# Layer 1 of a two-layer image kernel: four columns per transfer, even and odd columns apart in memory

## The chip, the cores and the metric

The kernel runs on one core of one Trainium2 chip. The metric is device time in microseconds (us). Before the change three runs took 5861.34, 5883.06 and 5891.94 us; their median, 5883.06 us, is the time before.

## What is computed

The input `x` has the shape (4, 64, 256, 256): batch, channels, height, width. Two layers follow each other, both with a residual:

```python
x = x + _L0_conv_ref(_gn(x), ...)   # layer 0
x = x + _L1_conv_ref(_gn(x), ...)   # layer 1
```

`_gn` is a group norm with 32 groups of two channels, over a whole image. Layer 0 is a pointwise convolution to 384 channels, a 3x3 convolution per channel, a product of q and k in the frequency domain of 8x8 patches, a layer norm over channels, a product with v, and a projection back to 64 channels. Layer 1 is a recurrence over the 256 columns of the image:

```python
def step(prev_col, cur_col):
    nb = jnp.concatenate([pad, prev_col, pad], axis=1)
    x = jnp.concatenate([nb[:, :-2], nb[:, 1:-1], nb[:, 2:]], axis=-1)
    new = _gru_cell(x.reshape(B * H, 3 * Cf), cur_col.reshape(B * H, Cf), w_ih, w_hh, b_ih, b_hh)
    return (new, new)
```

Each pixel's new state is that of a GRU cell. Its input is the states of three neighbouring pixels in the column before; its old state is the normalized pixel itself. Column 0 is passed on as it is. Column w needs column w-1, so the columns can only be worked off in order.

## The kernel before

All arithmetic is in float32. The width is the outer pixel dimension in memory, so that a column of 256 pixels of one channel is a run of 1 KB. Layer 0 writes its result to `x1`, a tensor in device memory of the shape [B, C, W, H] (line 185), and layer 1 reads it from there and writes `out` in the same layout.

*Order.* Nearly every instruction is recorded by the helper `InOrder` (line 145), which keeps each engine's instructions in program order. The profile therefore shows line 157 for almost everything, and groups are told apart by the names of their tiles. DMAs on the SP queue (`nc.sync.dma_start`) are issued in program order too: an instruction on SP that waits holds up all that come after it.

*Layer 0* (lines 271 to 694) runs over 32 blocks of the image. In each block, TensorE (PE) computes the hidden channels of the block (`pointwise`), applies matrices that are streamed in from `t_all` 24 times per block (`transform`, `values`; tile `t`, four buffers, SP queue), multiplies spectra on VectorE (tiles `pr`), and goes back (`inverse`). `finish` (line 608) gates and projects in four steps u: it loads the input again (tile `xr`, two transfers of 256 KB), adds the projection, takes statistics and stores the sum to `x1` by `store` (line 589), two transfers of 256 KB in runs of 512 B. The tiles `xr`, `pr`, `q`, `y` and `seen` share a pool of seven buffers (`wk`), so that a product may have to wait until a store of an `xr` has landed.

*Layer 1* (from line 717) holds columns in pieces of WB = 8. A column has 4 images x 64 channels; the 128 partitions hold two images at a time, and the second index (the slot) takes the other two. In even columns the slots hold images (0, 1) and (2, 3), in odd columns (0, 2) and (1, 3) (`SLOTS`, line 699). The pieces are

- `raw`: the columns as read, three buffers of 8 columns. `load_columns` (line 732) fetches two columns at a time, w and w+1: one transfer of 256 KB for the even column and two of 128 KB for the odd one, 16 columns ahead.
- `xn`: the columns normalized by ScalarE (ACT), `normalize` (line 748), one slot of one column in each half of a step, eight columns ahead. Before the loop it is done for nine columns.
- `xt`: the same with the halves of the partitions exchanged, made by two transfers of 128 KB each time two columns are normalized (the "turn").
- `st`: the states. `column` (line 801) computes a column in two parts along its height. The cut between the parts moves by one pixel per column, over 32 columns (`parts`, line 779), so that the first part of a column needs only the first part of the column before.

For each part, PE does the gates r, n and z (tiles `pshr`, `psni`, `pshz`, and `pshn` for both parts together) from `xn`, `xt` and the three shifted views of the previous `st`. `state` (line 838) then takes sigmoids and a tanh on ACT, and VectorE (DVE) combines them to the new state. GpSimd (POOL) adds the state to `raw` in place (`add`, line 767). After each odd column, `add` stores two columns to `out`: one transfer of 256 KB and two of 128 KB. The step then ends by loading two more columns. In SP's queue the order for each two columns is therefore: two turns, three stores, three loads.

Of the kernel before, what the change touches and what calls it, by code (L numbers as in the profile page):

```python
# [10 lines left out]
F32 = mybir.dt.float32  # L11
AF = mybir.ActivationFunctionType
ALU = mybir.AluOpType
# [3 lines left out]
B, C, W, H = 4, 64, 256, 256  # L17
HID = 6 * C
E = 2 * C
P = 128  # L20
NPAIR = B // 2
# [141 lines left out]
def tile_conv_then_gru(  # L163
# [17 lines left out]
    nc = InOrder(tc, tc.nc)  # L181

    const = ctx.enter_context(tc.tile_pool(name="const", bufs=1))
    dram = ctx.enter_context(tc.tile_pool(name="dram", bufs=1, space=DRAM))
    x1 = dram.tile([B, C, W, H], F32, tag="x1", name="x1")


    t_all = dram.tile([3, 8, HALO, 16 * NS], F32, tag="t_all", name="t_all")
# [28 lines left out]
    with tc.tile_pool(name="xa", bufs=3) as xa, tc.tile_pool(name="sta", bufs=1) as sta, tc.tile_pool(  # L217
        name="bps", bufs=1, space=PSUM
# [10 lines left out]
        for i in range(32):  # L229
            kind, s = i // 16, i % 16  # L230
            c0, num = 2 * P * kind, 2 * P - P * kind
            ps = banks[0:HALO, 4 * (i % 2) : 4 * (i % 2) + 4, 0:num]
            for k in range(4):
                at = slice(32 * k, 32 * k + 9)
# [25 lines left out]
    for a in range(2):  # L260
        at = slice(a * C, (a + 1) * C)
# [12 lines left out]
    with ExitStack() as s:  # L274
# [6 lines left out]
        place = [0]  # L281
# [307 lines left out]
        def store(n, u, xr):  # L589
            b, r0, c0 = n // 8, (n % 8) * 32 + (u // 2) * 8, (u % 2) * P  # L590
            for g in range(2):
                nc.sync.dma_start(
                    x1[b, :, r0 + 16 * g : r0 + 16 * g + 8, c0 : c0 + P],
                    xr[g * C : (g + 1) * C],
                )

        def look(n, k, t):

# [25 lines left out]
        for n in range(NBLK + 1):  # L624
# [13 lines left out]
            more = n // 8 + 1 < B  # L638
# [77 lines left out]

    WB = 8
    with ExitStack() as s:
        rawp = s.enter_context(tc.tile_pool(name="raw", bufs=3))
        colp = s.enter_context(tc.tile_pool(name="cols", bufs=2))  # L720
        gk = s.enter_context(tc.tile_pool(name="gk", bufs=2))
        ps_g = s.enter_context(tc.tile_pool(name="ps_g", bufs=1, space=PSUM))
        raws, xns, xts, stcols = {}, {}, {}, {}

        def columns(m, w):

            yield m[:, :, w, :].rearrange("(k a) c h -> (a c) k h", k=NPAIR), slice(0, P), 0
            for half in range(2):
                b0 = SLOTS[1][0][half]
                yield m[b0 : b0 + 2, :, w + 1, :].rearrange("b c h -> c b h"), slice(half * C, half * C + C), 1  # L730

        def load_columns(w):
            n, i = w // WB, w % WB
            if i == 0:
                raws[n] = rawp.tile([P, 2, WB, H], F32, tag="raw", name=f"raw_{n}")
            for of, at, j in columns(x1, w):
                nc.sync.dma_start(raws[n][at, :, i + j], of)

        def new_columns(n):
            xns[n] = colp.tile([P, 2, WB, H], F32, tag="xn", name=f"xn_{n}")  # L740
            xts[n] = colp.tile([P, WB, H], F32, tag="xt", name=f"xt_{n}")

        def empty_states(n):
            stcols[n] = st = colp.tile([P, 2, WB, H + 2], F32, tag="st", name=f"st_{n}")
            nc.gpsimd.memset(st[:, :, :, 0:1], 0.0)
            nc.gpsimd.memset(st[:, :, :, H + 1 : H + 2], 0.0)

        def normalize(w, slot):
            n, i = w // WB, w % WB
            if i == slot == 0:  # L750
                new_columns(n)
            nc.scalar.activation(
                xns[n][:, slot, i],
                raws[n][:, slot, i],
                AF.Identity,
                bias=sc1[:, w % 2, slot, 0:1],
                scale=sc1[:, w % 2, slot, 1:2],
            )
            if slot and i % 2:

                for half in range(2):
                    nc.sync.dma_start(
                        xts[n][half * C : (half + 1) * C, i - 1 : i + 1],
                        xns[n][(1 - half) * C : (2 - half) * C, half, i - 1 : i + 1],
                    )

        def add(w):
            n, i = w // WB, w % WB
            nc.gpsimd.tensor_tensor(
                raws[n][:, :, i], raws[n][:, :, i], stcols[n][:, :, i, 1 : H + 1], ALU.add  # L770
            )
            if i % 2:
                for of, at, j in columns(out, w - 1):
                    nc.sync.dma_start(of, raws[n][at, :, i - 1 + j])

        QUARTERS = ((0, 0), (0, 1), (1, 0), (1, 1))
        SKEW = 32

        def parts(w):


            at = H // 2 + SKEW // 2 - (w - 1) % SKEW
            return (0, at), (at, H)

        MAX = H // 2 + SKEW // 2

        def bank_pair(gate, w):
            return ps_g.tile([P, 2, 512], F32, tag=gate, name=f"ps{gate}_{w}")

        def quarters(ps, weights, rhs, start, stop):  # L790
            for r, c in QUARTERS:
                nc.tensor.matmul(
                    ps[c * C : (c + 1) * C, r],
                    lhsT=weights[r * C : (r + 1) * C],
                    rhs=rhs(r, c),
                    start=start,
                    stop=stop,
                    tile_position=(r * C, c * C),
                )

        def column(w):

            i, xn, xt, st = w % WB, xns[w // WB], xts[w // WB], stcols[(w - 1) // WB]

            def own(ps, gate, h0, h1, stop):

                quarters(
                    ps,
                    wh[:, gate, :],
                    lambda r, c: (xn[:, c] if r == c else xt)[r * C : (r + 1) * C, i, h0:h1],  # L810
                    True,
                    stop,
                )

            def taps(ps, gate, h0, h1, start):
                for t in range(3):
                    quarters(
                        ps,
                        wi[:, 3 * gate + t, :],
                        lambda r, c: st[r * C : (r + 1) * C, c, (w - 1) % WB, h0 + t : h1 + t],  # L820
                        start and t == 0,
                        t == 2,
                    )

            pn = bank_pair("hn", w)[:, :, 0:H]
            for part in range(2):
                h0, h1 = parts(w)[part]
                pr, pi, pz = (bank_pair(gate, f"{w}_{part}")[:, :, 0 : h1 - h0] for gate in ("hr", "ni", "hz"))
                own(pr, 0, h0, h1, False)
                taps(pr, 0, h0, h1, False)  # L830
                if part == 0:
                    own(pn, 2, 0, H, True)
                taps(pi, 2, h0, h1, True)
                own(pz, 1, h0, h1, False)
                taps(pz, 1, h0, h1, False)
                state(w, part, pn[:, :, h0:h1], pr, pi, pz)

        def state(w, part, pn, pr, pi, pz):
            h0, h1 = parts(w)[part]
            i, num = w % WB, h1 - h0  # L840
            xn, st = xns[w // WB], stcols[w // WB]
            g = gk.tile([P, 2, MAX], F32, tag=f"g{part}", name=f"g_{w}_{part}")[:, :, 0:num]
            n = gk.tile([P, 2, MAX], F32, tag=f"n{part}", name=f"n_{w}_{part}")[:, :, 0:num]
            z = gk.tile([P, 2, MAX], F32, tag=f"z{part}", name=f"z_{w}_{part}")[:, :, 0:num]
            nc.scalar.activation(g, pr, AF.Sigmoid, bias=b_rz[:, 0:1], scale=1.0)
            if w + WB < W:
                normalize(w + WB, part)
            nc.vector.scalar_tensor_tensor(n, pn, bias_sb[:, 5:6], g, ALU.add, ALU.mult)
            nc.vector.tensor_tensor(n, pi, n, ALU.add)

            nc.scalar.activation(z, pz, AF.Sigmoid, bias=b_rz[:, 1:2], scale=-1.0)
            nc.scalar.activation(n, n, AF.Tanh, bias=bias_sb[:, 2:3], scale=1.0)
            nc.vector.scalar_tensor_tensor(g, z, -1.0, xn[:, :, i, h0:h1], ALU.add, ALU.mult)
            nc.vector.tensor_tensor(n, n, z, ALU.mult)
            nc.vector.tensor_tensor(st[:, :, i, 1 + h0 : 1 + h1], n, g, ALU.subtract)

        for w in range(0, 2 * WB, 2):
            load_columns(w)
        for w in range(WB + 1):
            for slot in range(2):  # L860
                normalize(w, slot)
        empty_states(0)
        nc.vector.tensor_copy(stcols[0][:, :, 0, 1 : H + 1], xns[0][:, :, 0])
        for w in range(W):
            n, i = w // WB, w % WB
            if i == 0 and n + 1 < W // WB:
                empty_states(n + 1)
            if w:
                column(w)
            add(w)  # L870
            if i % 2 and w + 2 * WB < W:
                load_columns(w + 2 * WB - 1)


# [52 lines left out]
```

## Time and profile before

| | |
|---|---|
| median of three runs | 5883.06 us |
| profiled execution | 5869.95 us |
| its span, first to last instruction | 5868.2 us |
| granted TensorE clock, mean | 0.994 |
| end of layer 0's last projection on PE | about 4326 us |
| first load of `raw` issued | 4338.1 us |
| first matmuls of column 1 on turned columns | 4357.8 us |
| last add on POOL starts | 5858.9 us |

The profile lists, for each engine, its busy time and what ended its idle stretches. "Issue" stands for idle time in which an engine waited for nothing that the profile shows. PEld is PE's loading of weights, which lies beside the matmuls. A matmul in float32 appears as two records, so that the 92 matmuls of a column are 184 records. The granularity of the DMA lines is one packet; transfers on SP are `SPq`.

In layer 1, between 4400 and 5800 us, the DMA moved 160.97 MB in 151538 packets at a mean of 115 GB/s, 40.1% of the 16 engines' time on SP's queue and 1.7% on the instruction queue.

### The profile page before, as it was taken

Reading aid. Unit: us, or ns where it says so; the run is one execution under the profiler, and the core shown is the slowest. Engines: PE = TensorE matmul, PEld = TensorE weight load, DVE = VectorE, ACT = ScalarE, POOL = GpSimd, SP = SyncE. Lnnn points to the kernel's source line nnn. Section 1 sums busy time; section 2 is a strip of 40 time slices with the busy share of each in tenths; the row PEclk is TensorE's granted clock in tenths of the full one; section 3 lists DMA queues with packets and bytes.
Section 4 is the critical chain, followed back from the end, with each engine's and each line's share of the span. In section 5 each row is a group of like instructions: output and inputs, shape, how many; then the busy total and the mean of one; then the engine's idle time right before and its main releaser. Section 6 shows DMA issues by size and latency. Waiting matters only on the chain. (4 is left out here: it accounts for less than half of the span.)

```text
span 5868.2 us, 278629 instructions
## 1 busy us (share of the span) xinstructions
PE 5479.9 (93%) x127196; PEld 4762.6 (81%) x127196; DVE 4080.5 (70%) x9593; ACT 3475.4 (59%) x4604; POOL 500.8 (9%) x797
## 2 busy tenths in 40 slices
PE   2999999999999999999999999999979999999998
PEld 1878888888788878887888888878868888888888
DVE  2776777777767777777677767766667777776766
ACT  2556566665565656655655666556556666666655
POOL 0000000000000000000000000000002122222222
PEclk9999999999999999999999999999989999999999
DMA  8455555555555555555555454544444444444443
GB/s 225 135 156 147 151 151 155 154 142 152 157 147 154 150 151 159 141 150 159 150 152 150 140 143 126 142 139 125 137 114 116 116 116 117 115 117 113 116 114 81
DMA packets 561916, 818.04 MB, mean 139 GB/s; under 512 B 41353, under 2 KB 435373, under 8 KB 559677
## 3 DMA queue, kind: packets, MB, share of 16 engines
q1 hardware_dynamic: 520152, 633.59, 40.0%
q0 software_dynamic: 37776, 165.24, 9.5%
q8 instruction: 996, 16.32, 1.2%
q10 hardware_dynamic: 2808, 1.38, 0.1%
q14 instruction: 184, 1.50, 0.1%
HBM read 622.46 MB, written 144.05 MB: 131 GB/s over the span
## 5 line engine op out<-in xcount | busy, mean ns | idle before, releaser
L157 PEld LDWEIGHTS psring<-h,t 100*32 100x32 f32 x40960 | 1334.1, 115 | 294.0 <-issue 175.2
L157 PE MATMUL psring<-h,t 100*32 100x128 f32 x40960 | 1445.2, 274 | 105.9 <-issue 37.7
L157 PE MATMUL psring<-w_sb,xq 64*100 64x128 f32 x24576 | 1403.2, 271 | 55.7 <-POOL xq L157 40.2
L157 PEld LDWEIGHTS psring<-w_sb,xq 64*100 64x100 f32 x24576 | 1357.6, 164 | 117.0 <-issue 50.2
L157 ACT COPY h<-psring 100x1024 f32<-100x1024 f32 x1274 | 1205.5, 1027 | 161.4 <-PE psring L157 155.2
L157 DVE TENSOR_TENSOR pr<-psring,q 128x512 f32<-128x512 f32 (+1 forms) x576 | 463.3, 857 | 308.8 <-PE psring L157 234.8
L157 DVE BATCH_NORM_STATS2 lnst<-z 128x6 f32<-128x64 f32 x4096 | 545.4, 214 | 117.6 <-ACT z L157 117.6
L157 DVE TENSOR_TENSOR z<-z,lnm 128x1024 f32<-128x1024 f32 x512 | 612.7, 1218 | 8.8
L157 ACT COPY q<-psring 128x1024 f32<-128x1024 f32 x256 | 259.3, 1013 | 596.8 <-PE psring L157 358.9
L157 ACT ACTIVATE z<-pshz,b_rz 128x288 f32<-128x288 f32 (+7 forms) x510 | 242.6, 476 | 519.8 <-PE pshz L157 519.7
L157 PE MATMUL pshr<-st,wi 64*64 64x144 f32 (+7 forms) x12240 | 510.5, 270 | 34.9 <-issue 20.9
L157 PE MATMUL psni<-st,wi 64*64 64x144 f32 (+7 forms) x12240 | 510.4, 270 | 24.4 <-issue 22.4
L157 PE MATMUL pshz<-st,wi 64*64 64x144 f32 (+7 forms) x12240 | 510.8, 270 | 23.1 <-issue 21.9
L157 ACT COPY z<-psring 128x2048 f32<-128x2048 f32 x128 | 238.9, 1867 | 446.7 <-PE psring L157 441.7
L157 PE MATMUL psring<-pr,g_sb 32*64 32x512 f32 x8192 | 494.8, 594 | 5.7 <-issue 5.5
L157 ACT ACTIVATE y<-psring,ln_sb 128x512 f32<-128x512 f32 x512 | 372.5, 781 | 200.5 <-PE psring L157 197.0
L157 PEld LDWEIGHTS psni<-st,wi 64*64 64x64 f32 x12240 | 446.5, 133 | 45.5 <-issue 34.4
L157 PEld LDWEIGHTS pshr<-st,wi 64*64 64x64 f32 x12240 | 422.3, 133 | 52.3 <-issue 49.5
L157 DVE COPY h<-psring 100x1024 f32<-100x1024 f32 x262 | 320.3, 1223 | 198.7 <-PE psring L157 194.7
L157 PEld LDWEIGHTS pshz<-st,wi 64*64 64x64 f32 x12240 | 424.9, 133 | 37.3 <-issue 36.4
L157 DVE SCALAR_TENSOR_TENSOR g<-z,xn 128x288 f32<-128x288 f32 (+7 forms) x510 | 218.4, 428 | 311.9 <-ACT z L157 310.0
L157 POOL TENSOR_TENSOR raw<-raw,st 128x512 f32<-128x512 f32 x256 | 303.7, 1186 | 1146.0 <-ACT xn L157 548.1
(98 smaller groups left out, 7377.9 us busy)
## 6 DMA issues: line engine op xcount, KB each, us to landing
t<-t_all SPq DMA_DIRECT2D x768, 400.0 KB
xq<-in_xh POOLq DMA_DIRECT2D x128, 800.0 KB, 4.6
xr<-in_x SPq DMA_DIRECT2D x256, 256.0 KB
x<-xr SPq DMA_DIRECT2D x256, 256.0 KB
seen<-in_x POOLq DMA_DIRECT2D x192, 256.0 KB, 4.1
raw<-x SPq DMA_DIRECT2D x128, 256.0 KB
raw<-x SPq DMA_DIRECT2D x256, 128.0 KB
xt<-xn SPq DMA_DIRECT2D x256, 128.0 KB
```

Source lines behind the costliest of these rows:

```text
L157: return self.tc.keep_in_program_order(got(*args, **kwargs))
```

## The change

Layer 1 loads, stores and turns four columns at a time. `x1` and `out` get a leading index for even and odd columns, so that two even (or two odd) columns lie side by side, as a run of 2 KB per channel; the host puts `out` back in order. Layer 0's `store` writes even and odd columns with separate transfers, four of 128 KB in place of two of 256 KB. `raw` becomes seven buffers of four columns, in the order even, even, odd, odd (`place`), and `xn` and `xt` follow the same order. One load is 512 KB (two even columns) or 256 KB (two odd columns, half the images), and stores are alike; a turn is 256 KB. Loads and stores are written at one per kind and step, three steps of each four. Before the loop, four columns are normalized instead of nine, and the first five steps normalize two columns each.

```diff
-    x1 = dram.tile([B, C, W, H], F32, tag="x1", name="x1")
+    x1 = dram.tile([2, B, C, W // 2, H], F32, tag="x1", name="x1")
...
             for g in range(2):
-                nc.sync.dma_start(
-                    x1[b, :, r0 + 16 * g : r0 + 16 * g + 8, c0 : c0 + P],
-                    xr[g * C : (g + 1) * C],
-                )
+                at = r0 // 2 + 8 * g
+                for odd in range(2):
+                    nc.sync.dma_start(x1[odd, b, :, at : at + 4, c0 : c0 + P], xr[g * C : (g + 1) * C, odd::2])
...
-        rawp = s.enter_context(tc.tile_pool(name="raw", bufs=3))
+        rawp = s.enter_context(tc.tile_pool(name="raw", bufs=7))
...
+        def place(w):
+            return w % WB // 4 * 4 + w % 2 * 2 + w % 4 // 2
+
+        def columns(m, w, i):
             if i == 0:
+                of = m[0, :, :, w // 2 : w // 2 + 2, :]
+                return of.rearrange("(k a) c w h -> (a c) k (w h)", k=NPAIR), raws[w // 4][:, :, 0:2]
+            half = i - 1
+            b0 = SLOTS[1][0][half]
+            of = m[1, b0 : b0 + 2, :, w // 2 : w // 2 + 2, :]
+            return of.rearrange("b c w h -> c b (w h)"), raws[w // 4][half * C : half * C + C, :, 2:4]
+
+        def load_columns(w, i):
+            if i == 0:
+                raws[w // 4] = rawp.tile([P, 2, 4, H], F32, tag="raw", name=f"raw_{w // 4}")
+            of, to = columns(x1, w, i)
+            nc.sync.dma_start(to.rearrange("p k w h -> p k (w h)"), of)
+
+        def store_columns(w, i):
+            to, of = columns(out, w, i)
+            nc.sync.dma_start(to, of.rearrange("p k w h -> p k (w h)"))
...
-            if slot and i % 2:
+            if slot and i % 4 == 3:
...
                     nc.sync.dma_start(
-                        xts[n][half * C : (half + 1) * C, i - 1 : i + 1],
-                        xns[n][(1 - half) * C : (2 - half) * C, half, i - 1 : i + 1],
+                        xts[n][half * C : (half + 1) * C, i - 3 : i + 1],
+                        xns[n][(1 - half) * C : (2 - half) * C, half, i - 3 : i + 1],
                     )
...
         def add(w):
-            if i % 2:
-                for of, at, j in columns(out, w - 1):
-                    nc.sync.dma_start(of, raws[n][at, :, i - 1 + j])
+            raw = raws[w // 4][:, :, place(w) % 4]
+            nc.gpsimd.tensor_tensor(raw, raw, stcols[w // WB][:, :, w % WB, 1 : H + 1], ALU.add)
...
-            if w + WB < W:
-                normalize(w + WB, part)
+            for more in range(ahead(w - 1), ahead(w)):
+                normalize(more, part)
...
+        def ahead(w):
+            return min(2 * w + 4, w + WB + 1, W)
...
             add(w)
-            if i % 2 and w + 2 * WB < W:
-                load_columns(w + 2 * WB - 1)
+            if i >= 2:
+                store_columns(w - i, i - 2)
+            elif i == 0 and w:
+                store_columns(w - 4, 2)
+            if i < 3 and w - i + 2 * WB < W:
+                load_columns(w - i + 2 * WB, i)
+        store_columns(W - 4, 2)
```

In the last part of the diff, `i` is w modulo 4.

More of the change, by code (lines that the diff above doesn't have):

```diff
@@ L723, in tile_conv_then_gru @@
         raws, xns, xts, stcols = {}, {}, {}, {}
[L725 to L733, printed above, removed]
-            if i == 0:
-                raws[n] = rawp.tile([P, 2, WB, H], F32, tag="raw", name=f"raw_{n}")
-            for of, at, j in columns(x1, w):
-                nc.sync.dma_start(raws[n][at, :, i + j], of)
+        def place(w):
+            return w % WB // 4 * 4 + w % 2 * 2 + w % 4 // 2
+        def columns(m, w, i):
+            if i == 0:
+                of = m[0, :, :, w // 2 : w // 2 + 2, :]
[12 more added lines that the diff above has]
+            nc.sync.dma_start(to, of.rearrange("p k w h -> p k (w h)"))
         def new_columns(n):
@@ L752, in normalize @@
             nc.scalar.activation(
-                xns[n][:, slot, i],
-                raws[n][:, slot, i],
+                xns[n][:, slot, place(w)],
+                raws[w // 4][:, slot, place(w) % 4],
                 AF.Identity,
@@ L758, in normalize @@
             )
-            if slot and i % 2:
+            if slot and i % 4 == 3:
                 for half in range(2):
                     nc.sync.dma_start(
-                        xts[n][half * C : (half + 1) * C, i - 1 : i + 1],
-                        xns[n][(1 - half) * C : (2 - half) * C, half, i - 1 : i + 1],
+                        xts[n][half * C : (half + 1) * C, i - 3 : i + 1],
+                        xns[n][(1 - half) * C : (2 - half) * C, half, i - 3 : i + 1],
                     )
         def add(w):
[L768 to L771, printed above, removed]
-            if i % 2:
-                for of, at, j in columns(out, w - 1):
-                    nc.sync.dma_start(of, raws[n][at, :, i - 1 + j])
+            raw = raws[w // 4][:, :, place(w) % 4]
+            nc.gpsimd.tensor_tensor(raw, raw, stcols[w // WB][:, :, w % WB, 1 : H + 1], ALU.add)
         QUARTERS = ((0, 0), (0, 1), (1, 0), (1, 1))
@@ L801, in column @@
         def column(w):
-            i, xn, xt, st = w % WB, xns[w // WB], xts[w // WB], stcols[(w - 1) // WB]
+            xn, xt, st = xns[w // WB], xts[w // WB], stcols[(w - 1) // WB]
             def own(ps, gate, h0, h1, stop):
@@ L809, in own @@
                     wh[:, gate, :],
-                    lambda r, c: (xn[:, c] if r == c else xt)[r * C : (r + 1) * C, i, h0:h1],
+                    lambda r, c: (xn[:, c] if r == c else xt)[r * C : (r + 1) * C, place(w), h0:h1],
                     True,
@@ L852, in state @@
             nc.scalar.activation(n, n, AF.Tanh, bias=bias_sb[:, 2:3], scale=1.0)
-            nc.vector.scalar_tensor_tensor(g, z, -1.0, xn[:, :, i, h0:h1], ALU.add, ALU.mult)
+            nc.vector.scalar_tensor_tensor(g, z, -1.0, xn[:, :, place(w), h0:h1], ALU.add, ALU.mult)
             nc.vector.tensor_tensor(n, n, z, ALU.mult)
             nc.vector.tensor_tensor(st[:, :, i, 1 + h0 : 1 + h1], n, g, ALU.subtract)
-        for w in range(0, 2 * WB, 2):
-            load_columns(w)
-        for w in range(WB + 1):
+        def ahead(w):
+            return min(2 * w + 4, w + WB + 1, W)
+        for w in range(0, 2 * WB, 4):
+            for i in range(3):
+                load_columns(w, i)
+        for w in range(ahead(0)):
             for slot in range(2):
@@ L864, in tile_conv_then_gru @@
         for w in range(W):
-            n, i = w // WB, w % WB
-            if i == 0 and n + 1 < W // WB:
+            n, i = w // WB, w % 4
+            if w % WB == 0 and n + 1 < W // WB:
                 empty_states(n + 1)
@@ L921 @@
         args.append(nc.dram_tensor(f"in_{name}", v.shape, mybir.dt.from_np(v.dtype), kind="ExternalInput").ap())
-    args.append(nc.dram_tensor("out_0", (B, C, W, H), F32, kind="ExternalOutput").ap())
+    args.append(nc.dram_tensor("out_0", (2, B, C, W // 2, H), F32, kind="ExternalOutput").ap())
     with tile.TileContext(nc) as tc:
@@ L925 @@
     r = run_bass_kernel_spmd(nc, [feeds], core_ids=[0])
-    return np.ascontiguousarray(r.results[0]["out_0"].transpose(0, 1, 3, 2))
+    got = r.results[0]["out_0"].reshape(2, B, C, W // 2, H)
+    return np.ascontiguousarray(got.transpose(1, 2, 4, 3, 0).reshape(B, C, H, W))
```

## The prediction

> **What bounds the kernel now.** I read the page's busy shares and slices first, then what PE waits for in the stage that the change rewrites (layer 1, from 4358 us, where the first column starts, to the end), then the stretches around single waits, then SP's timeline. From the page:
>
> ```profile
> PE 5479.9 (93%) x127196; PEld 4762.6 (81%) x127196; DVE 4080.5 (70%) x9593; ACT 3475.4 (59%) x4604; POOL 500.8 (9%) x797
> DMA  8455555555555555555555454544444444444443
> q1 hardware_dynamic: 520152, 633.59, 40.0%
> q8 instruction: 996, 16.32, 1.2%
> ```
>
> PE is the bound in both layers. DMA is half busy on average, so its mean bandwidth binds nothing; only where transfers bunch can it matter. The waits of PE from 4358 us to the end (total us, times, longest):
>
> ```profile
> PE pshr L157 <- issue: 29.0, 60, 1.2
> PE pshz L157 <- issue: 28.7, 53, 1.2
> PE psni L157 <- issue: 22.4, 31, 1.7
> PE pshr L157 <- DMA xt<-xn: 14.1, 1, 14.1
> PE pshr L157 <- DVE st L157: 13.4, 7, 1.9
> ```
>
> PE hardly ever waits for data: 13.4 us at the seven turns of the skew, and once for the first turned columns. The largest item, 80 us in 144 waits, is "issue": nothing that the profile tracks was missing. Where they sit names them. From the middle of one such wait to the middle of the next, PE executes a multiple of 128 matmuls (columns: stretch, length, PE busy, matmuls, clock, DMA share, GB/s):
>
> ```profile
> 4894.57:4902.36 7.79, 7.60 (x256) 1.00 0.44 123
> 4902.36:4906.36 4.00, 3.79 (x128) 1.00 0.37 103
> 4906.36:4914.17 7.81, 7.62 (x256) 1.00 0.46 123
> 4914.17:4918.17 4.00, 3.82 (x128) 1.00 0.37 102
> ```
>
> 128 matmuls with their 128 weight loads are 256 instructions, and queue q8 moved 16.32 MB in 996 packets, 16.4 KB each: PE waits for its next block of instructions. Counting on in 128s gives 338 block ends between 4409 and 5800 us, 3.87 us of work apart; 140 of them have a wait. Whether one has it depends on the DMA share in the 4 us that end 1 us before it:
>
> ```profile
> 4880.80:4884.80 4.00, 3.59 (x130) 1.00 0.17 42
> 4884.57:4888.57 4.00, 4.00 (x151) 1.00 0.66 185
> 4901.25:4905.25 4.00, 3.82 (x136) 1.00 0.38 107
> 4978.78:4982.78 4.00, 4.00 (x145) 1.00 0.73 206
> ```
>
> The block end at 4885.80 has no wait, that at 4889.57 waits 1.08 us, at 4906.25 0.23 us, at 4983.78 1.18 us. Over all 338, with the share from half-microsecond stretches: share under 0.3, 66 ends, mean wait 0.01 us; 0.3 to 0.6, 197 ends, 0.15 us; over 0.6 (mean 0.68), 75 ends, 0.64 us. A busy DMA delays the block, and PE stands still. So what the change does to layer 1's time is what it does to the bunching of its transfers. SP's timeline (start, length, transfers):
>
> ```profile
> 4899.37 3.26 SPq L157 DMA_DIRECT2D xt<-xn  x2
> 4902.72 5.17 SPq L157 DMA_DIRECT2D out<-raw  x3
> 4907.95 2.25 SPq L157 DMA_DIRECT2D raw<-x  x3
> ```
>
> Each pair of columns brings eight transfers of 128 or 256 KB, held apart by waits: the two turns by ACT's two slots, the second and third store by POOL's add. No stretch of 4 us is fully busy.
>
> [...] loads of 1 KB packets filled the DMA at 257 GB/s (4340 to 4356 us), and 1 KB and 2 KB packets cost about 57 and 120 ns. Doubling the runs thus saves no DMA time.
>
> **The change part by part.** *Arithmetic of layer 1.* Same matmuls, VectorE operations and adds; nothing gained.
>
> *SP's issues.* Per four columns 16 become 8, at 0.52 to 0.64 us each. SP is not on the path, so nothing is gained directly.
>
> *Bunching.* Bytes are equal: 2560 KB (of 1024) per four columns, 10.2 us at 257 GB/s of a cycle of 4 x 5.88 = 23.5 us. But SP runs its queue in order and stops only where an instruction must wait. Loads wait for nothing recent (the pool now holds seven blocks, and the stores of a reused block lie eight columns back). So they don't stay in "their" step: SP's order is two turns, [add of column 3] odd store, odd store, even load, odd load, [add of column 2] even store, odd load, and again. After the add of column 3, 256+256+512+256 KB go out in four issues, some 2.5 us, for 5.1 us of DMA work. Three columns later, after the add of column 2, follow 512+256 KB and right behind them both turns of 256 KB, which were nearly ready: another 5.1 us. Taking the add to end 9.6 us after its column starts on PE, as for the column whose xt issues at 4899.37 and 4902.11 lie 2.45 and 5.2 us after its start, the second group starts about 5.8 us before the next first one. The two join to about 10.7 us of full DMA, then 12.8 us of quiet. There are 5.7 block ends per cycle after it is lengthened a little. An end has a share over 0.6 if its 4 us overlap the full stretch by 2.4 or more: 10.7 + 4 - 4.8 = 9.9 us of 23.5, or 2.4 ends; a share of 0.3 to 0.6 for 2.4 us, 0.6 ends. The wait at full share isn't shown. The lower bound is 0.64 us (share 0.68). The upper one continues the line from 0.15 (mean share 0.41) to 0.64 (0.68): 1.8 us per unit, 1.2 us at 1.0. I take 0.75, near the lower one, since a wait also lengthens the cycle and drains the queue. Then 2.4 x 0.75 + 0.6 x 0.15 = 1.89 us per cycle, and 64 cycles make 121 us for 80: **+41 us** (bounds +24 and +110).
>
> *Larger packets.* A block on an engine busy with 2 KB or 4 KB packets might wait longer. Against it: around the turns, 2 KB already, block ends wait no longer than around 1 KB loads. Priced at 0, inside the upper bound.
>
> *Start of layer 1.* PE idled 14.1 us for the first xt, behind 24 loads (15.05 us on SP). Twelve loads issue in 7 us, and ACT normalizes 4 columns first instead of 9 (8 x 0.59 us for 18). But the same 4 MB drain at 257 GB/s, and the first turn is 512 KB where the first pair was 256: 1 us more. Against slow issuing at the beginning this is -1 us (-4 to +1). ACT then does two columns a step for five steps: 0.59 us more between a part's two sigmoids; ACT idled 0.9 to 1.2 us there on PE. Hidden.
>
> *Tail.* One issue less after the last add: -0.6 us; 512 KB still go out.
>
> *Layer 0.* 256 stores of 256 KB become 512 of 128 KB: 0.6 us more SP per extra one, 4.8 us in a block of about 127 us. Behind them in SP's queue stand the next xr loads and four t fetches; PE waited only 15 us for t there. DMA is full in this stretch (216 to 276 GB/s from 1334 to 1340 us), so issuing later mostly doesn't land later. But VectorE's products already wait 68.4 us in 23 places for a store to land, and PE's inverse waits for them. I take 4 us (0, to 1 us in each of 31 blocks, 31).
>
> Sum: 41 - 1 - 1 + 4 = +43 us. On the profiled execution (5869.95 us, span 5868.2) that is 5913. That execution lies 13 us under the median of the runs; against the median, 5883 + 43 = **5926 us**.
>
> **The rivals.**
> 1. *Bunching costs* (the forecast): own range 5900 to 5990. Chance 0.50.
> 2. *Requests count, not bytes* (the other side, faster): if each transfer disturbs block fetches by its start, layer 1's waits go with its number, 1024 before, 512 after, and half of the 80 us goes: 5883 - 40 - 2 = 5841. It decides once the wait in full stretches stays under 0.4 us. For it: the quiet half of each cycle has no waits. Against: waits follow the share, which is bytes. 0.18.
> 3. *Neither*: the joined groups come apart, or the wait is capped, so that the sum stays near 80 us: 5883 - 2 + 4 = 5885. For it: POOL's add moves by a microsecond or two between columns. 0.20.
> 4. *The block waits for the whole queue*: it now reaches 2.6 us of work (1310 KB less 2.5 us of draining), on average some 1.3, before about 0.4. Then 0.9 us more in 2 ends a cycle, 115 us: 6040. Against: at 1337 us of layer 0 the queue was as deep and PE kept running. 0.12.
>
> **How the numbers follow.** About 0.5% (29 us) is what a measurement of this kernel can tell from no change; the three runs lie 0.5% apart. Slower by more: 0.38 of the first, all of the fourth, 0.05 of the third, 0.55. Faster: 0.14 of the second, 0.02 of the first, 0.16. The rest, 0.29, is within it. The range, 5845 to 5990, leaves out the fourth and the lower part of the second.
>
> **What would show it.** In layer 1, PE's "issue" waits near 120 us, in fewer places, longer ones above 1 us common; DMA slices unchanged in the mean, but stretches of 4 us at a share near 1.0 followed by some 12 us near 0; SP's transfers in two groups of four per four columns. Right at the start, the wait for xt stays within a few us of 14.1. In layer 0, the wait of pr for the stores of x grows by at most 30 us. The forecast is wrong if the issue waits fall below 80 us, or if PE waits for xt or raw in mid-layer.

## The result, and the profile after

The changed kernel took 5937.61 us (median of four runs, 5932.63 to 5953.08) beside 5879.14 us for the kernel before. The ratio is 1.0097, with a 95% interval from 1.0075 to 1.0118: slower by about 57 us.

The same lines of the page, changed kernel:

```profile
PE 5471.9 (92%) x127196; PEld 4774.2 (80%) x127196; DVE 4081.0 (69%) x9593; ACT 3472.0 (59%) x4604; POOL 499.3 (8%) x797
DMA  8455555555555555555555555545454433334442
q1 hardware_dynamic: 442328, 633.57, 39.8%
q8 instruction: 996, 16.32, 1.2%
```

PE does the same work in the same busy time, within 8 us. The DMA moves the same bytes in fewer packets, and its busy share has hardly moved. So neither work nor traffic was added; PE stands still longer. The waits of PE in layer 1, from 4381 us to the end (total us, times, longest):

```profile
PE pshr L157 <- issue: 45.0, 46, 2.1
PE psni L157 <- issue: 42.8, 35, 2.3
PE pshz L157 <- issue: 39.6, 42, 1.9
PE pshr L157 <- DVE st L157: 13.4, 7, 1.9
PE pshr L157 <- DMA xt<-xn: 11.6, 2, 11.2
PE pshn L157 <- issue: 2.0, 3, 0.8
```

The issue waits, at the ends of the instruction blocks, sum to 129 us in 126 places, where they were 80 us in 145. There are fewer, and they are longer. What waits for data has not grown.

That these are waits for instruction blocks can be read from the packets of the instruction queue q8 (16 KB each, one per block: 996 packets beside 127196 matmuls, 127.7 matmuls to a packet), whose start and end the traces keep. Over ten traces, this one, that of before and those of the experiments below, there are 919 issue waits above 0.3 us in layer 1, and every one ends 1.2 to 1.75 us (median 1.4) after such a packet has ended. The packet itself takes 1.1 us in the mean, whether PE waits for it or not. What differs is its start: in the changed kernel about 1 us into the block that PE is working on where there is next to no wait after it (under 0.1 us), and 2.6 us into it where the wait is above 0.5 us. With 3.87 us of work in a block, 1.1 us for the packet and 1.4 us after it, a packet may start about 1.4 us into the block before PE has to wait (an estimate from these numbers). So the blocks don't travel more slowly; they start late. What holds them back is the question of the experiments.

SP's timeline for one cycle of four columns (start, length, transfers) shows what the queue holds at that time:

```profile
4900.51 0.38 SPq L157 DMA_DIRECT2D out<-raw  x1
4900.94 0.60 SPq L157 DMA_DIRECT2D raw<-x  x1
4901.63 3.05 SPq L157 DMA_DIRECT2D xt<-xn  x2
4905.99 1.33 SPq L157 DMA_DIRECT2D out<-raw  x2
4907.36 1.90 SPq L157 DMA_DIRECT2D raw<-x  x2
4924.81 0.39 SPq L157 DMA_DIRECT2D out<-raw  x1
```

Two groups of 1280 KB follow each other within 9 us; then SP issues nothing for 15 us (between 4400 and 5800 us SP waited 1032.2 us for POOL's adds to `raw`, up to 18.3 us at a time; before 354.2 us, up to 4.8). The second group is handed out in 3.3 us, at 390 KB/us (KB of 1024 bytes). Three stretches of 4 us, each ending 1 us before a block's end (columns: stretch, length, PE busy, matmuls, clock, DMA share, GB/s):

```profile
4946.50:4950.50 4.00, 3.96 (x139) 1.00 0.07 25
4908.51:4912.51 4.00, 3.31 (x118) 1.00 0.88 267
4950.33:4954.33 4.00, 4.00 (x151) 1.00 1.03 299
```

The block end at 4951.50 has no wait, that at 4913.51 waits 1.22 us, and that at 4955.33 1.03 us. Over 339 ends: share under 0.3, 186 ends, mean wait 0.01 us; 0.3 to 0.6, 31 ends, 0.24 us; 0.6 to 0.8, 53 ends, 0.72 us; over 0.8, 69 ends, 1.14 us.

By stages, from the traces: layer 1's first load was issued at 4361.5 us (4338.1 before), so layer 0 and the passage to layer 1 took 23.4 us more. From there to the first matmul on turned columns it was 19.0 us (19.6 before). From that matmul to the end of the span it was 1551.2 us (1510.4 before), 40.8 us more. The issue waits grew by 49 us; PE's busy time in layer 1 is 5.7 us shorter (1395.5 us, 1401.2 before), and gaps too short to be listed make up most of the rest.

### The profile page after: what moved, and what is told of

Its sections match the earlier page's. It is cut to its first block, busy times and chain, and to the rows that moved or that the text cites. A ratio compares the mean times of both kernels' runs of the same rounds, so it can differ in the third digit from the quotient of the medians.

```text
span 5931.7 us, 278258 instructions
## 1 busy us (share of the span) xinstructions
PE 5471.9 (92%) x127196; PEld 4774.2 (80%) x127196; DVE 4081.0 (69%) x9593; ACT 3472.0 (59%) x4604; POOL 499.3 (8%) x797
## 4 chain that ended last, share of the span: by engine, by line
PE 46%; issue 3%; DMA 2%; ACT 1%; DVE 1%; SPq 1%; POOLq 0%; ACTq 0%; DVEq 0%
PE psring L157 23%; PE pshz L157 8%; PE pshr L157 8%; PE psni L157 6%; DMA t<-t_all 2%; PE pshn L157 2%; SPq L157 1%; ACT v L157 1%; ACT z L157 0%; DVE z L157 0%; DVE xr L157 0%; ACT h L157 0%; DMA xt<-xn 0%; DVE lnst L157 0%; DMA raw<-x 0%
## 5 line engine op out<-in xcount | busy, mean ns | idle before, releaser
L157 PE MATMUL pshr<-st,wi 64*64 64x144 f32 (+7 forms) x12240 | 507.8, 271 | 41.0 <-issue 26.7
L157 PEld LDWEIGHTS psni<-st,wi 64*64 64x64 f32 x12240 | 449.3, 133 | 64.6 <-issue 53.6
```

The lines of the kernel that those rows point to most:

```text
L157: return self.tc.keep_in_program_order(got(*args, **kwargs))
```

## The experiments

Each ran beside the kernel before on the same chip; ratios are to it, with 95% intervals. "Issue waits" are PE's in layer 1, from each kernel's one profiled execution; those of bunched_halves and spread_halves lay 15 and 19 us under the medians of their kernels, those of before and changed 6 to 16 and 4 us under, that of split_store 9 us over, so that small differences in this column say little.

| kernel | median us | ratio (interval) | issue waits us |
|---|---|---|---|
| before | 5876.25 to 5885.89 | 1 | 80 |
| changed | 5937.61 | 1.0097 (1.0075 to 1.0118) | 129 |
| split_store | 5887.54 | 1.0019 (1.0009 to 1.0028) | 84 |
| bunched_halves | 5866.12 | 0.9978 (0.9965 to 0.9992) | 73 |
| spread | 5895.15 | 1.0028 (1.0018 to 1.0039) | 99 |
| no_out | 5814.72 | 0.9885 (0.9863 to 0.9907) | 38 |
| halves | 5878.09 | 0.9982 (0.9971 to 0.9993) | 66 |
| spread_halves | 5864.03 | 0.9951 (0.9934 to 0.9968) | 54 |
| quarters | 5916.00 | 1.0043 (1.0028 to 1.0058) | 20 |
| act_loads | 5892.92 | 1.0017 (1.0004 to 1.0030) | 88 |

**Is it the DMA at all?** The kernel `no_out` leaves out the stores of all columns but the last eight.

```diff
-            if i % 2:
+            if i % 2 and w + WB > W:
                 for of, at, j in columns(out, w - 1):
```

> The kernel before, leaving out the stores of out for all columns but the last eight, so 40% of layer 1's DMA bytes; all arithmetic stays. Theory: the issue waits come from DMA traffic; with a mean share near 0.26 in place of 0.42 few stretches reach 0.6, and they fall from 80 us to under 30 us: about 50 us faster than before. Rival (PE's own sequencer needs this time at each block, whatever the DMA does): issue waits stay near 80 us and the time stays.

The mean share fell to 0.26, the issue waits to 38 us (under 30 were expected), and the time by 61 us (ratio 0.9885). So at least half of these waits come from the transfers. The waits fell by 42 us and the time by more: PE's busy time in layer 1 fell too, from 1401.2 to 1384.4 us. Why the same matmuls took less is not shown.

**Layer 0's store alone.** `split_store` is the kernel before with

```diff
-                nc.sync.dma_start(
-                    x1[b, :, r0 + 16 * g : r0 + 16 * g + 8, c0 : c0 + P],
-                    xr[g * C : (g + 1) * C],
-                )
+                for odd in range(2):
+                    nc.sync.dma_start(
+                        x1[b, :, r0 + 16 * g + odd : r0 + 16 * g + 8 : 2, c0 : c0 + P],
+                        xr[g * C : (g + 1) * C, odd::2],
+                    )
```

> The kernel before with one part of the change alone: layer 0's store of even and odd columns by separate transfers, four of 128 KB for two of 256 KB, to the same places as before. Theory: SP issues 2.6 us of stores where it issued 1.3, and the t fetches behind them in its queue come later. PE's waits for t go from 15 us to about 41 us, as in the changed kernel, layer 1 starts some 20 us later, and its issue waits stay at 80 us: about 20 us slower than before. Rival: layer 0's 23 us between the two profiled executions are chance, or come from writing x1 in two halves of memory: then within 8 us of before and t waits near 15 us.

It is slower by 1.0019, 11 us (5 to 16). In its trace layer 1 starts at 4359.0 us. That is no chance of one execution: in the four profiles with split stores (changed, split_store, halves, act_loads) the first load is issued at 4359.0 to 4364.2 us, in the six without at 4334.7 to 4347.0 us. PE's waits for t were 26.7 us (15.2 before, 41.0 changed), where about 41 had been expected, and the products' waits for a store to land 90.2 us (68.4 before, 82.9 changed). Single traces scatter here: over the six without split stores the waits for t are 15.2 to 23.9 us and those for a store 64.6 to 68.4; over the four with them, 26.7 to 41.0 and 82.9 to 90.2. SP's timeline in layer 0, before and then changed:

```profile
2109.94 2.24 SPq L157 DMA_DIRECT2D xr<-in_x  x2
2114.09 1.28 SPq L157 DMA_DIRECT2D x<-xr  x2
2115.41 5.05 SPq L157 DMA_DIRECT2D t<-t_all  x3
```

```profile
2118.28 1.31 SPq L157 DMA_DIRECT2D xr<-in_x  x2
2120.85 3.15 SPq L157 DMA_DIRECT2D x<-xr  x4
2124.09 3.13 SPq L157 DMA_DIRECT2D t<-t_all  x3
```

From the start of the first store in the row to the first t it is 1.32 us before and 3.24 us after. The traces give layer 0 some 22 us more on average, the timing of this kernel 11; which is nearer stays open.

**The bunching alone.** `bunched_halves` has the changed kernel's layer 1 step by step, but the layout of before, and for each transfer two of half the size.

```diff
         def columns(m, w, i):
+            raw = raws[w // 4]
+            for j in (0, 2):
+                if i == 0:
+                    yield m[:, :, w + j, :].rearrange("(k a) c h -> (a c) k h", k=NPAIR), raw[:, :, j]
+                else:
+                    b0 = SLOTS[1][0][i - 1]
+                    at = slice((i - 1) * C, i * C)
+                    yield m[b0 : b0 + 2, :, w + j + 1, :].rearrange("b c h -> c b h"), raw[at, :, j + 1]
...
+                    for j in (i - 3, i - 1):
+                        nc.sync.dma_start(
+                            xts[n][half * C : (half + 1) * C, j : j + 2],
+                            xns[n][(1 - half) * C : (2 - half) * C, half, j : j + 2],
+                        )
```

> The changed kernel's layer 1 in its order of steps, but with the layout and the transfers of before: each transfer of the changed kernel is two of half the size, runs of 1 KB (turns 2 KB), and layer 0 stores as before. Theory (bunching): issue waits of PE in layer 1 stay near the changed kernel's 129 us, since the same bytes go out in the same two joined groups; layer 0 as before; about 40 us slower than before, 20 us faster than the changed kernel. Rival (larger packets or larger transfers hold the instruction blocks up): issue waits fall to about 80 us and the time to that of before.

The theory failed here. The groups are joined as in the changed kernel, but for one store of 256 KB, which already goes out behind the group before (the last line):

```profile
4911.45 3.47 SPq L157 DMA_DIRECT2D xt<-xn  x4
4914.97 3.27 SPq L157 DMA_DIRECT2D out<-raw  x4
4918.29 2.44 SPq L157 DMA_DIRECT2D raw<-x  x4
4920.95 0.41 SPq L157 DMA_DIRECT2D out<-raw  x1
```

Yet the issue waits are 73 us. At a share of 0.6 to 0.8, 135 block ends wait 0.41 us on average, where the changed kernel's wait 0.72. So the DMA's share in the 4 us ahead doesn't decide alone. Two differences were left: packets of 1 KB for 2 KB, and requests of half the size.

**Spreading the same requests.** `spread` is the kernel before with each column's store and one column's load after its own add.

```diff
-            if i % 2:
-                for of, at, j in columns(out, w - 1):
-                    nc.sync.dma_start(of, raws[n][at, :, i - 1 + j])
+            for of, at, j in columns(out, w - i % 2):
+                if j == i % 2:
+                    nc.sync.dma_start(of, raws[n][at, :, i])
...
-            if i % 2 and w + 2 * WB < W:
-                load_columns(w + 2 * WB - 1)
+            if w - i % 2 + 2 * WB < W:
+                load_columns(w - i % 2 + 2 * WB, (1, 2) if i % 2 else (0,))
```

> The kernel before with the same transfers spread over the steps: after each column's add its own store and the load of one column, so that SP waits between them; even columns one load of 256 KB, odd columns two of 128 KB (raw in four buffers). Theory (share in the 4 us ahead of a block's end): no stretch is over 0.6 for long, waits about 0.15 us at each of 365 block ends, 55 us for 80: about 25 us faster than before. Rival (the waits follow bytes or requests in all, not their bunching): both are the same as before, so issue waits near 80 us and the time within 8 us of before.

It went the other way: issue waits 99 us, slower by 1.0028. Only 49 ends had a share over 0.6, but they waited 1.07 us each. SP's timeline shows what lies ahead of them:

```profile
4901.78 0.38 SPq L157 DMA_DIRECT2D out<-raw  x1
4902.20 0.47 SPq L157 DMA_DIRECT2D raw<-x  x1
4902.77 1.40 SPq L157 DMA_DIRECT2D xt<-xn  x2
```

The store and load of 256 KB each and two turns of 128 KB go out in 2.4 us, 320 KB/us. The DMA moved 257 GB/s, or 251 KB/us, with loads alone (4340 to 4356 us of the kernel before; with stores among them it reached 299 GB/s in a stretch above), so a queue forms (the count further down has over 300 KB at 80 of 343 block ends), with packets no longer than before. The new theory: a block is held up by the *depth* of the queue it meets, that is, by requests handed out faster than the DMA works them off. SP needs about 0.6 us for most requests of layer 1, large or small (medians of 0.47 to 0.71 us by kind and size; 0.38 us for the stores of even columns in this kernel and the changed one), so small requests pace themselves (128 KB in 0.6 us are 213 KB/us, less than the 251 of the loads).

**Depth against packet length.** `halves` is the changed kernel with each transfer of layer 1 in two: loads and stores by the index k, turns by partitions. Layout, runs and steps stay.

```diff
-            nc.sync.dma_start(to.rearrange("p k w h -> p k (w h)"), of)
+            for k in range(2):
+                nc.sync.dma_start(to.rearrange("p k w h -> p k (w h)")[:, k], of[:, k])
...
+                    for c in (0, C // 2):
+                        nc.sync.dma_start(
+                            xts[n][half * C + c : half * C + c + C // 2, i - 3 : i + 1],
+                            xns[n][(1 - half) * C + c : (1 - half) * C + c + C // 2, half, i - 3 : i + 1],
+                        )
```

> The changed kernel with each transfer of layer 1 issued as two halves: same layout, same runs of 2 KB (turns 4 KB), same steps; sixteen requests of 128 and 256 KB per four columns for eight of 256 and 512 KB. Theory (queue depth): SP spends about 0.6 us per request, so it can hand out at most some 260 KB/us, as fast as the DMA moves it, and no long queue forms ahead of an instruction block: layer 1's issue waits fall from 129 us to about 75 us, as in the bunched kernel with small transfers, some 45 us faster than the changed kernel and 10 us slower than before (layer 0's split stores stay). Rival (long packets hold the instruction blocks up): waits stay near 129 us and the time near 1.010 of before.

Issue waits 66 us for 129, and 0.9982 of before in place of 1.0097, though layer 0's split stores are still in it. The group that went out in 3.3 us now takes 6.8, 190 KB/us:

```profile
4910.69 2.46 SPq L157 DMA_DIRECT2D xt<-xn  x4
4913.25 3.23 SPq L157 DMA_DIRECT2D out<-raw  x4
4916.52 3.48 SPq L157 DMA_DIRECT2D raw<-x  x4
```

and PE's waits in layer 1 are

```profile
PE pshr L157 <- issue: 31.0, 56, 1.6
PE pshz L157 <- issue: 24.2, 45, 1.2
PE pshr L157 <- DVE st L157: 13.3, 7, 1.9
PE psni L157 <- issue: 10.0, 23, 1.2
```

Packets of 2 and 4 KB are thus not the cause: with requests of the same sizes, `bunched_halves` had 73 us with packets of 1 and 2 KB. The size of a request is what was changed, and with it the rate at which bytes are handed out; the two can't be told apart by this run. `spread_halves` does the same to `spread`, only for the even columns:

```diff
                 if k in which:
-                    nc.sync.dma_start(raws[n][at, :, i + j], of)
+                    for s in range(2) if k == 0 else [slice(0, 2)]:
+                        nc.sync.dma_start(raws[n][at, s, i + j], of[:, s])
```

(and alike for the store).

> The spread kernel with the store and the load of an even column issued as two halves of 128 KB each; all packets and steps as in the spread kernel, whose issue waits were 99 us. There two 256 KB requests followed each other within 0.9 us. Theory (queue depth): with 128 KB per 0.5 us the queue stays short; issue waits fall to about 65 us, some 30 us faster than the spread kernel. Rival (what counts is where in the step the transfers lie, or the bytes in the 4 us ahead): both are unchanged, so waits stay near 99 us and the time near 1.003 of before.

The group of 768 KB takes 3.1 us instead of 2.4:

```profile
4901.55 0.82 SPq L157 DMA_DIRECT2D out<-raw  x2
4902.41 0.94 SPq L157 DMA_DIRECT2D raw<-x  x2
4903.45 1.15 SPq L157 DMA_DIRECT2D xt<-xn  x2
```

At 252 KB/us it just keeps to the 251 KB/us of the loads. Issue waits 54 us, and 0.9951 of before (0.9934 to 0.9968), the lowest ratio of all kernels here that compute everything.

The packet records let the queue be counted: the bytes of the requests that SP has issued, less those of its packets that have ended. The count goes back to 0 in the quiet stretches. Mean wait at a block's end, in us, by the queue 3.5 us before that end (in brackets the number of ends):

```
queue, KB        to 100      to 200      to 300      to 400      over 400
before           0.03 (101)  0.12 (105)  0.25  (50)  0.55  (92)  0.27   (2)
changed          0.01 (207)  0.28   (5)  0.35  (11)  0.39   (4)  1.04 (113)
bunched_halves   0.01 (163)  0.14  (31)  0.23  (96)  0.49  (25)  0.78  (39)
spread           0.05  (97)  0.05 (104)  0.26  (62)  0.87  (39)  0.88  (41)
halves           0.02 (173)  0.21  (35)  0.26  (87)  0.36  (23)  0.60  (39)
spread_halves    0.04  (83)  0.12 (130)  0.24 (139)  0.00   (3)    -
```

From 200 to 300 KB the five kernels with 50 ends or more agree within 0.03 us, whatever their packets. Above that they don't all agree: at 300 to 400 KB `spread` waits 0.87 us (39 ends) and `halves` 0.36 us (23 ends), so depth is not the whole answer; what else matters stays open. It is a better measure than the share, though. If one takes the wait for each depth from before and changed alone, it gives 77 us for `bunched_halves` (71 measured at these ends), 85 for `spread` (95), 75 for `halves` (66) and 48 for `spread_halves` (53). The share in the 4 us ahead, used in the same way, gives 117, 67, 119 and 68. With the depth 3.0 us before the end it is 80, 80, 83 and 70. For `no_out` and, further down, `act_loads` the depth gives too much (53 and 104 us, 36 and 86 measured).

The wait does not grow with the whole queue: in the changed kernel it is 0.83 us on average at 400 to 500 KB (21 ends) and 1.18 us over 800 KB (18 ends), where the 300 KB or more between them are over 1.2 us of work at 257 GB/s.

**Too many requests.** `quarters` splits every transfer of the kernel before in two (stores and turns like the loads shown).

```diff
-                nc.sync.dma_start(raws[n][at, :, i + j], of)
+                for k in range(2):
+                    nc.sync.dma_start(raws[n][at, k, i + j], of[:, k])
```

> The kernel before with every transfer of layer 1 issued as two halves (64 and 128 KB), steps and packets as before. Theory (queue depth): SP paces the DMA at about 150 KB/us, well under what it moves, so hardly any queue forms; issue waits fall from 80 us to 40 to 55 us, 25 to 40 us faster than before. Rival (the share in the 4 us ahead decides): the share evens out near 0.45, waits about 0.15 us at each end, 55 us. Rival (requests count): twice as many, waits grow above 100 us, slower than before.

The issue waits fell to 20 us, further than expected, and no share was over 0.6. But the kernel is slower. PE's longest waits in layer 1:

```profile
PE pshz L157 <- ACT z L157: 64.1, 53, 2.7
PE pshr L157 <- DMA xt<-xn: 26.3, 4, 25.0
PE pshr L157 <- DVE st L157: 16.7, 9, 2.5
PE pshr L157 <- issue: 9.1, 26, 0.7
```

With 16 requests for two columns SP is always issuing:

```profile
4909.68 4.77 SPq L157 DMA_DIRECT2D raw<-x  x6
4914.55 2.97 SPq L157 DMA_DIRECT2D xt<-xn  x4
4917.61 4.66 SPq L157 DMA_DIRECT2D out<-raw  x6
4922.32 4.43 SPq L157 DMA_DIRECT2D raw<-x  x6
```

The loads come late, ACT waits for them ahead of its sigmoids (188 us for raw between 4400 and 5800 us), and PE waits for ACT. SP has become the bound: from 4909.68 to 4926.75 us there is no gap of more than 0.1 us between these groups of issues. As PE now waits for other things too, its 20 us of issue waits can't be compared directly with those of the other kernels. The first columns, behind 48 loads, come 11 us later too.

**Joined groups or single large requests.** `act_loads` is the changed kernel with the loads after the first sixteen columns on ACT's queue.

```diff
-            nc.sync.dma_start(to.rearrange("p k w h -> p k (w h)"), of)
+            (nc.sync if w < 2 * WB else nc.scalar).dma_start(to.rearrange("p k w h -> p k (w h)"), of)
```

> The changed kernel with the loads of layer 1 (all after the first sixteen columns) issued from ACT's queue at the end of their steps; SP keeps stores and turns, and sizes stay. The loads no longer follow the stores at once, so the two groups of four are pulled apart. Theory (queue depth): one load of 512 KB is 2 us of DMA work by itself, handed out in one request, so blocks still meet deep queues: issue waits stay above 100 us (129 in the changed kernel), time within 15 us of the changed kernel, 1.007 to 1.012 of before. Rival (it is the joining of the groups that makes the queue deep, single large requests are harmless): waits fall to 80 us or less, 45 us faster than the changed kernel. In both, if ACT's three more instructions per four columns delay its chain, PE waits for ACT z appear.

Issue waits 88 us, 1.0017: between the two expectations, nearer to the rival. A load of 512 KB alone does less than I expected; large requests one right behind the other build the deep queue. By the count of packets, on both queues together, more than 400 KB were open 3.5 us before 68 of 352 block ends, in the changed kernel before 113 of 340. One such load is a queue of 500 KB for a moment only (an estimate: at 251 KB/us its 512 KB are worked off in 2 us), and I had priced it too high. The loads also have a queue of their own here; what of the 41 us comes from that was not tested.

## Why the prediction was right, and where not

*The time.* 5926 us was forecast, 5937.61 measured; +43 us forecast, +57 (44 to 69) measured.

*Layer 1.* +41 us forecast for the waits of PE at block ends, 121 us against 80. The trace has 129 against 80, and layer 1 took 40.8 us more. The two groups per cycle came as described, with 15 us of silence between. But the sum came out with some luck. At a share over 0.6 it had 2.4 ends per cycle at 0.75 us each; the trace has 122 of 339 ends there, about 2.1 per cycle, at 0.96 us in the mean. The price near the lower bound was too low, the number of ends too high, and the two errors mostly cancel.

*The reason given for it.* The step "what the change does to layer 1's time is what it does to the bunching of its transfers" failed as stated. The same groups in small requests cost nothing (`bunched_halves`), and spreading large ones cost something (`spread`). In its place the runs show the size of the requests handed out in a row, and the count of the packets points to the depth of the queue that they build (over 400 KB at 113 of 340 block ends in the changed kernel, at 2 of 350 before). In the kernel before, share and depth went together: block ends with a share under 0.3, of 0.3 to 0.6 and over 0.6 had about 10, 180 and 350 KB open in the mean, 3.5 us ahead. In the changed kernel they go together again (about 0 and 265 KB in the first two classes, 450 KB at 0.6 to 0.8, 670 KB over 0.8), and the line of wait against share carried on to 1.14 us over 0.8. The number was right by a quantity that stood in for the cause.

*SP's issues.* "Nothing is gained directly" from half as many: SP is not on the path, true (0% of the chain that ended last, on the page of before); but the step missed that these 0.6 us per request had held the queue short: with twice the issues, `halves` has about half the waits (66 us for 129) and over 400 KB open at 39 block ends in place of 113.

*Larger packets.* Priced at 0; `halves` beside `bunched_halves` (66 and 73 us, packets twice as long in the first) shows that this was right. Nor did the DMA gain by them: over layer 1, two 1 KB packets of SP's queue took 112 ns before (56 ns each in the mean), a 2 KB packet 111 ns in the changed kernel.

*Start and tail.* -1 us forecast for the start, -0.6 us in the traces. For the tail -0.6 us was forecast; from the start of POOL's last add to the end of the span it is 9.2 us, 9.3 before.

*Layer 0.* This is the term that was mis-sized: 4 us forecast (0 to 31), 11 us timed alone, 22 us in the traces. The mechanism was the one named, stores ahead of t fetches on SP and products that wait for stores. "Issuing later mostly doesn't land later" was too hopeful: PE's waits for t are 12 us longer in the mean of the traces with split stores (31 us for 19), the products' waits for a store 20 us (87 for 66).

*The rivals.* Fewer requests making it faster has the wrong sign: twice as many, in `halves`, took 63 us of waits away. "Neither" is excluded by 129 us. The rival of the whole queue named the right quantity with too high a price: the mean wait is 1.18 us over 800 KB. What was held against it stands in the trace of before: from 1336 to 1340 us PE was busy for 4.00 us of 4.00 at a DMA share of 1.03.

## What to carry to other kernels

When PE waits for nothing that the profile shows, count its instructions between the waits: if it is a block each time (128 matmuls and their weight loads here), look at what the DMA queue holds a few microseconds earlier (3.5 us here). Larger transfers were no gain by themselves where nothing waited for data (ratio 1.0097). Hold what a queue issues in a row against what the DMA moves: here, with 251 KB/us for the loads alone, the same 1280 KB handed out at 390 KB/us went with 129 us of waits, at 190 KB/us with 66. Requests whose issue takes as long as their transfer kept the queue short: in `spread_halves`, 128 KB per 0.5 us, which at 251 KB/us is also 0.5 us of transfer (an estimate), it was over 300 KB at 3 of 355 block ends, with 54 us of waits. The other end is near: with twice the requests of before, in `quarters`, the issuing engine became the bound (1.0043).

## What I had not expected of the hardware

Among the loads of layer 1, the cost of an issue on SP hardly depends on the size: medians of 0.61 us for 512 KB (changed), 0.59 us for 256 and 0.61 us for 128 KB (before), 0.59 us for 64 KB (`quarters`). It does depend on the transfer: a t of 400 KB takes 0.27 us (median of 768, before and changed). And an instruction block's delay grows much less than the queue: 1.18 us on average over 800 KB in the changed kernel, where the longest wait is 2.3 us; the longest of all traces is 2.7 us, in `spread`.
